# Layer 1's running maximum, taken by VectorE from each PSUM bank of scores

## The chip, the cores and the metric

The program runs on one core of a Trainium2 chip. A core has five engines that run their own instruction queues in order: TensorE (PE; its weight loads are listed apart as PEld), VectorE (DVE), ScalarE (ACT), GpSimd (POOL) and SyncE (SP, which here only issues DMAs). TensorE writes into PSUM, eight banks of 512 fp32 numbers on each of 128 partitions; VectorE and ScalarE read it. The metric is the device time of one execution in microseconds, the median of several runs.

## The reference, cut to what matters

Four layers follow each other on an image batch of shape (4, 64, 64, 128): a 7x7 neighbourhood attention, a full attention, a gated projection with a layer norm, and a selective scan in four directions. The change touches the second, "layer 1":

```python
def _L1_conv_ref(x, gn_scale, gn_bias, wq, bq, wk, bk, wv, bv, wo, bo):
    B, H, W, C = x.shape
    N = H * W
    h = group_norm(x, gn_scale, gn_bias)
    hf = h.reshape(B, N, C)
    q = hf @ wq + bq
    k = hf @ wk + bk
    v = hf @ wv + bv
    w_ = jnp.einsum('bqd,bkd->bqk', q, k) * C ** (-0.5)
    w_ = jax.nn.softmax(w_, axis=2)
    o = jnp.einsum('bqk,bkd->bqd', w_, v)
    o = o @ wo + bo
    return x + o.reshape(B, H, W, C)
```

With N = 4096 positions per image, the scores are a 4096 x 4096 matrix per image. Everything is fp32. The softmax over the keys needs the largest score of each query.

## The kernel before, in words

The function `layers_0_to_2` goes through the four images one after the other. Per image it runs layer 0, then layer 1 with layer 2 and the front of layer 3 woven into it; `layer_3` follows at the end for all images.

Layer 1 (the function `layer_1`) takes 32 blocks of 128 queries. The scores of a block are held transposed: keys on the partitions, queries along the free dimension, 32 key tiles of 128 x 128 in one SBUF tile `st` (L606). They are made in eight groups of four key tiles. For a group, `score` lets TensorE do four matmuls (L613) into one PSUM bank `ps`, and ScalarE copies the bank into `st` (L616). The banks come from a ring of four (`ps_s`), which layer 2's and layer 3's matmuls share.

The maximum of each query over all keys is found in steps:

- VectorE takes the elementwise maximum over key tiles in SBUF, once four groups are there: tiles 0 to 7 against 8 to 15 at group 3 (L618), then the running maximum `mx` of eight tiles against the next eight at groups 5 and 7 (L620).
- `fold` brings the eight tiles down to one with three maxima of 512, 256 and 128 elements (L625).
- `soften` lets TensorE transpose that tile (L630, into `pt`). VectorE reduces it to minus the maximum of each query (L632, `nm`), multiplies the identity by it (L634, `dm`), and TensorE multiplies a matrix of ones with that (L636, into `pb`), which gives a bank in which every partition has minus the maximum of each query. VectorE adds it to `st` in two halves (L639) and ScalarE takes the exponential of each (L640).

`value` multiplies the exponentials with the values, whose extra column of ones gives the sum (L646), and `finish` divides and adds to `xt` (L650, L651).

The loop over i runs three blocks at once: it makes the scores of block i, softens block i-1, and takes the values of block i-2. `fold` of block i-1 stands at the head of iteration i, `soften` ahead of group 2. Behind each block, `between(i)` adds a slice of layer 2 (four kinds of slice in turn: `turn`, `mix`, `add`, `norm`, L685 to L747) and of the front of layer 3 (projections L786, gates L815, convolution taps on ScalarE, GpSimd and VectorE, L829 to L865, and more). So a cycle of four blocks repeats. TensorE's stream in a block is, group by group, four score matmuls and four value matmuls.

The order on each engine isn't simply the order of the calls: except where `keep_in_program_order` pins an instruction, the framework's scheduler arranges each engine's queue, and it adds the waits between engines. It also keeps two engines from one PSUM bank.

Of the kernel before, what the change touches and what calls it, by code (L numbers as in the profile page):

```python
# [22 lines left out]
F32 = mybir.dt.float32  # L23
AF = mybir.ActivationFunctionType
ALU = mybir.AluOpType
# [4 lines left out]
P = 128  # L30
B, H, W, C = 4, 64, 64, 128
L = H * W
NT = L // P
# [105 lines left out]
def layers_0_to_2(  # L139
    ctx, tc, xf, mata, matb, rows, rpb, convw, sel, ident, cl, dram, big, ring, early, x3_d, ub_d, zf_d, y_d, dbl_d, ct_d, gw_d, bw_d  # L140
):
    nc = tc.nc
    wp = ctx.enter_context(tc.tile_pool(name="wa", bufs=1))
    tmp = ctx.enter_context(tc.tile_pool(name="tmp", bufs=2))
# [5 lines left out]
    def ps_s(shape, name):  # L150
        return psp.tile(shape, F32, name=name, tag="s", bufs=4)

    def ps_t(shape, name):
        return psp.tile(shape, F32, name=name, tag="t", bufs=2)

    def ps_o(shape, name):
        return psp.tile(shape, F32, name=name, tag="o", bufs=2)
# [11 lines left out]
    def m(name, p=P):  # L169
        a, e = MA[name]  # L170
        return ma[0:p, a:e] if e <= nma else once[0:p, a - nma:e - nma]
# [73 lines left out]
    ones = wp.tile([P, P], F32, name="ones")  # L245
# [308 lines left out]
    def layer_1(b, xt, hT, st, between):  # L554
        mv = sml.tile([P, 2], F32, name="mv1", tag="mv1", bufs=1)
        nc.vector.bn_aggr(mv, st)

        pm = ps_o([P, 1], "pm")
        nc.tensor.matmul(pm, lhsT=m("group"), rhs=mv[:, 0:1], start=True, stop=True)
        gm = sml.tile([P, 1], F32, name="gm", tag="gm", bufs=1)  # L560
        nc.vector.tensor_copy(gm, pm)
        dv = sml.tile([P, 1], F32, name="dv", tag="dv", bufs=1)
        nc.vector.tensor_tensor(dv, mv[:, 0:1], gm, ALU.subtract)
        vv = sml.tile([P, 1], F32, name="vv", tag="vv", bufs=1)
        nc.vector.scalar_tensor_tensor(vv, dv, dv, mv[:, 1:2], ALU.mult, ALU.add)
        pvar = ps_o([P, 1], "pvar")
        nc.tensor.matmul(pvar, lhsT=m("group"), rhs=vv, start=True, stop=True)
        sd = sml.tile([P, 1], F32, name="sd", tag="sd", bufs=1)
        nc.vector.tensor_scalar(sd, pvar, 1e-6, None, ALU.add)
        nc.scalar.activation(sd, sd, AF.Sqrt)  # L570
        ga = sml.tile([P, 1], F32, name="ga", tag="ga", bufs=1)
        nc.vector.reciprocal(ga, sd)
        nc.vector.tensor_tensor(ga, ga, cl("gn_s"), ALU.mult)

        qT = big.tile([P, L], F32, name=f"qT1_{b}", tag="qT")
        kT = big.tile([P, L], F32, name=f"kT1_{b}", tag="kT")

        v = big.tile([P, NT, C + 1], F32, name=f"v1_{b}", tag="v")
        nc.gpsimd.memset(v[:, :, C:C + 1], 1.0)
        for n in range(NCH):  # L580
            cs = bass.ts(n, CH)
            nc.vector.tensor_scalar(hT[:, cs], hT[:, cs], gm, ga, ALU.subtract, ALU.mult)
            pq = ps_s([P, CH], "pq1")
            nc.tensor.matmul(pq, lhsT=m("wq"), rhs=hT[:, cs], start=True, stop=True)
            nc.scalar.activation(qT[:, cs], pq, AF.Identity, bias=bqk[:, 0:1], scale=C ** -0.5)
            pk = ps_s([P, CH], "pk1")
            nc.tensor.matmul(pk, lhsT=m("wk"), rhs=hT[:, cs], start=True, stop=True)
            nc.scalar.activation(kT[:, cs], pk, AF.Identity, bias=bqk[:, 1:2])
            pv = ps_s([P, 4, C], "pv1")
            for k in range(4):  # L590
                nc.tensor.matmul(pv[:, k, :], lhsT=hT[:, bass.ts(4 * n + k, P)], rhs=wvo, start=True, stop=True)
            nc.vector.tensor_tensor(
                v[:, 4 * n:4 * n + 4, 0:C], pv, vrow.unsqueeze(1).to_broadcast([P, 4, C]), ALU.add
            )

        G = 4

        class Block:
            pass

        def start(i):
            k = Block()
            k.st = ring([P, NT, P], "st")  # L606
            k.mx = tmp.tile([P, 2 * G, P], F32, name="mx1", tag="mx1")
            return k

        def score(i, k, g):  # L610
            ps = ps_s([P, G, P], "sc1")
            for r in range(G):
                nc.tensor.matmul(  # L613
                    ps[:, r, :], lhsT=kT[:, bass.ts(G * g + r, P)], rhs=qT[:, bass.ts(i, P)], start=True, stop=True
                )
            nc.scalar.copy(k.st[:, G * g:G * g + G, :], ps)  # L616
            if g == 3:
                nc.vector.tensor_tensor(k.mx, k.st[:, 0:8, :], k.st[:, 8:16, :], ALU.max)  # L618
            elif g in (5, 7):
                nc.vector.tensor_tensor(k.mx, k.mx, k.st[:, 4 * g - 4:4 * g + 4, :], ALU.max)  # L620

        def fold(k):
            mx = k.mx
            for n in (4, 2, 1):
                nc.vector.tensor_tensor(mx[:, 0:n, :], mx[:, 0:n, :], mx[:, n:2 * n, :], ALU.max)  # L625

        def soften(k):
            mx = k.mx
            pt = ps_t([P, P], "pt1")
            nc.tensor.transpose(pt, mx[:, 0, :], ident)  # L630
            nm = sml.tile([P, 1], F32, name="nm1", tag="nm1")
            nc.vector.tensor_reduce(nm, pt, AX.X, ALU.max, negate=True)  # L632
            dm = tmp.tile([P, P], F32, name="dm1", tag="dm1")
            nc.vector.tensor_scalar(dm, ident, nm, None, ALU.mult)  # L634
            pb = ps_t([P, P], "pb1")
            nc.tensor.matmul(pb, lhsT=ones, rhs=dm, start=True, stop=True)  # L636
            for h in range(2):
                part = k.st[:, 16 * h:16 * h + 16, :]
                nc.vector.tensor_tensor(part, part, pb.unsqueeze(1).to_broadcast([P, 16, P]), ALU.add)  # L639
                nc.scalar.activation(part, part, AF.Exp)  # L640

        def value(k, g):
            if g == 0:
                k.po = ps_o([P, C + 1], "po1")
            for j in range(G * g, G * g + G):
                nc.tensor.matmul(k.po, lhsT=k.st[:, j, :], rhs=v[:, j, :], start=(j == 0), stop=(j == NT - 1))  # L646

        def finish(i, k):
            ri = sml.tile([P, 1], F32, name="ri1", tag="ri1")
            nc.vector.reciprocal(ri, k.po[:, C:C + 1])  # L650
            nc.vector.scalar_tensor_tensor(xt[:, i, :], k.po[:, 0:C], ri, xt[:, i, :], ALU.mult, ALU.add)  # L651

        blocks = {}
        for i in range(NT + 2):
            if 0 < i <= NT:
                fold(blocks[i - 1])
            if i < NT:
                blocks[i] = start(i)
            for g in range(NT // G):

                if 0 < i <= NT and g == (2 if i < NT else 0):
                    soften(blocks[i - 1])
                if i < NT:
                    score(i, blocks[i], g)
                if i >= 2:
                    value(blocks[i - 2], g)
            if i >= 2:
                finish(i - 2, blocks.pop(i - 2))
            between(i)
# [440 lines left out]
    for b in range(B):  # L1110
# [5 lines left out]
        def between(i):  # L1116

            n, part = divmod(i - 6, 4)
            if i == 6 and b + 1 < B:
                ahead.append(load_x(b + 1))  # L1120
            if i >= 6 and n < NCH:
                parts[part](n)
            first_part(i)
            if b + 1 < B and i == NT + 1:
                edge_of[b + 1] = edge_bias(0)
            if b + 1 < B and i == NT + 3:
                bias_m[:] = bias_tiles()
                for t, d in zip(bias_m, bias_d):
                    nc.sync.dma_start(t, d)

        first_part = front(b)
        first_part(-1)
        layer_1(b, xt, *handed.pop(b), between)
        if b + 1 < B:
            coming = layer_0(b + 1, ahead[0], edge_of[b + 1])
# [385 lines left out]
```

## Time and profile before

| | us |
|---|---|
| median of 3 runs | 3769.5 (3767.92 to 3772.58) |
| the profiled execution | 3760.92 |
| its span, first to last instruction | 3759.1 |
| VectorE's maxima of 1024 elements, L618: 128 of them | 162.1 |
| the folds L625: 384 of them, 655 ns mean | 251.5 |
| the score matmuls L613, first to last | 233.9 to 3037.2 |

The mean granted clock of TensorE was 0.921 of full speed, and 0.98 to 1.00 in the stretches of layer 1. The chain of work that ended last, by engine and by line:

```profile
PE 53%; DVE 22%; ACT 9%; POOL 6%; issue 6%; DMA 3%; SPq 1%; DVEq 0%; POOLq 0%; ACTq 0%
PE po L646 14%; PE sc L613 14%; DVE mx L625 4%; PE pt L493 4%; DVE acc L865 3%; POOL inp L1242 3%; DVE st L639 3%; PE sc L458 2%; PE po L504 2%; DVE mx L620 2%; POOL y L1284 2%; ACT st L640 2%; ACT st L616 2%; PE pp L514 1%; PE pz L815 1%
```

The rows of groups have the line, the engine, the operation, what it writes and reads, the shapes and the count; behind the first bar the busy time in us and the mean duration in ns; behind the second the time for which the engine stood idle ahead of these instructions, and what ended most of that. TensorE matmuls overlap each other, so their rate is read from the starts: eight records of 128 columns (four fp32 matmuls, each of two records) take 0.89 us. The trace has five stretches: the four images with layers 0 to 2 up to about 3060 us, each with its layer 1 of some 520 to 550 us, and layer 3 behind them.

### The profile page before, as it was taken

To read this page: it belongs to the slowest core of one execution; us is meant where nothing else is said; L and a number is where in the kernel's file an instruction comes from. 1 tells how busy PE (TensorE), PEld (TensorE's weight loads), DVE (VectorE), ACT (ScalarE), POOL (GpSimd) and SP (SyncE) were. 2 spreads that over 40 slices of the span, in tenths; PEclk is the share of its full clock that TensorE was granted. 3 is DMA by queue.
4 is the path that set the end of the run, shared out by engine and by line. 5 is a ranking of instruction groups with operands and counts; after the bars stand their busy time and mean duration, and the time that the engine had idled before them with its cause. 6 is when DMAs were issued, how large, how long until landed. Compare 5 with 4: busy or idle time off the path is not lost.

```text
span 3759.1 us, 69275 instructions
## 1 busy us (share of the span) xinstructions
PE 3353.6 (89%) x26774; PEld 2764.6 (74%) x26774; DVE 2812.2 (75%) x4843; ACT 2697.4 (72%) x4385; POOL 1447.7 (39%) x1592
## 2 busy tenths in 40 slices
PE   6999999999999999998999999989999987666647
PEld 3779989966799889667998897779988862222236
DVE  3667777766777788666777876667777867999968
ACT  3865667778676776786677777867767768999934
POOL 5500012245122122451222223522221337999856
PEclk8999999999999999999999999999999995555569
DMA  4100000131010012410121212100100259999998
GB/s 139 52 3 27 10 18 30 44 100 36 18 43 32 32 41 81 129 42 4 48 75 32 72 44 97 45 1 24 46 27 32 68 153 241 222 227 205 214 265 289
DMA packets 188301, 310.89 MB, mean 83 GB/s; under 512 B 22303, under 2 KB 110908, under 8 KB 183068
## 3 DMA queue, kind: packets, MB, share of 16 engines
q1 hardware_dynamic: 144068, 220.79, 17.4%
q0 software_dynamic: 24384, 76.95, 11.4%
q10 hardware_dynamic: 19520, 8.73, 0.8%
q8 instruction: 211, 3.46, 0.4%
q14 instruction: 118, 0.97, 0.1%
HBM read 167.69 MB, written 155.56 MB: 86 GB/s over the span
## 4 chain that ended last, share of the span: by engine, by line
PE 53%; DVE 22%; ACT 9%; POOL 6%; issue 6%; DMA 3%; SPq 1%; DVEq 0%; POOLq 0%; ACTq 0%
PE po L646 14%; PE sc L613 14%; DVE mx L625 4%; PE pt L493 4%; DVE acc L865 3%; POOL inp L1242 3%; DVE st L639 3%; PE sc L458 2%; PE po L504 2%; DVE mx L620 2%; POOL y L1284 2%; ACT st L640 2%; ACT st L616 2%; PE pp L514 1%; PE pz L815 1%
## 5 line engine op out<-in xcount | busy, mean ns | idle before, releaser
L646 PE MATMUL po<-v,st 128*128 128x129 f32 x8192 | 1076.3, 274 | 4.1 <-ACT st L640 4.1
L613 PE MATMUL sc<-qT,kT 128*128 128x128 f32 x8192 | 1075.6, 275 | 0.4 <-ACT st L616 0.4
L613 PEld LDWEIGHTS sc<-qT,kT 128*128 128x128 f32 x8192 | 997.7, 192 | 21.9 <-issue 19.0
L646 PEld LDWEIGHTS po<-v,st 128*128 128x128 f32 x8192 | 993.9, 191 | 5.4 <-issue 5.4
L616 ACT COPY st<-sc 128x512 f32<-128x512 f32 x1024 | 577.8, 583 | 499.4 <-PE sc L613 491.2
L639 DVE TENSOR_TENSOR st<-st,pb 128x2048 f32<-128x2048 f32 x256 | 573.8, 2282 | 46.2 <-PE pb L636 45.7
L620 DVE TENSOR_TENSOR mx<-mx,st 128x1024 f32<-128x1024 f32 x256 | 317.9, 1242 | 240.5 <-ACT st L616 238.4
L640 ACT ACTIVATE st<-st 128x2048 f32<-128x2048 f32 x256 | 482.7, 1908 | 9.5 <-DVE st L639 8.2
L1231 PE MATMUL pdt<-dbl,dt 8*128 8x512 f32 x512 | 307.3, 1081 | 144.1 <-ACT de L1238 141.9
L1242 POOL TENSOR_TENSOR inp<-de,ub 128x1024 f32<-128x1024 f32 x128 | 410.1, 4406 | 10.6 <-DMA ub_d<-u 6.4
L1231 PEld LDWEIGHTS pdt<-dbl,dt 8*128 8x128 f32 x512 | 114.2, 312 | 334.3 <-ACT de L1238 269.9
L710 POOL TENSOR_TENSOR x<-x,row 128x512 f32<-128x512 f32 x32 | 50.0, 1561 | 736.8 <-PE pt L275 736.8
L484 POOL TENSOR_SCALAR pr<-pr,sm 128x308 f32<-128x308 f32 (+3 forms) x512 | 243.6, 495 | 220.5 <-DVE sm L482 188.5
L856 POOL TENSOR_TENSOR gsum<-gsum,tp 128x504 f32<-128x504 f32 (+1 forms) x177 | 251.0, 1420 | 141.5 <-ACT gsum L844 81.5
L476 ACT ACTIVATE pr<-pr,mx 128x308 f32<-128x308 f32 (+3 forms) x512 | 262.6, 517 | 0.0
L625 DVE TENSOR_TENSOR mx<-mx 128x512 f32<-128x512 f32 (+2 forms) x384 | 251.5, 655 | 5.9
L1269 DVE TENSOR_TENSOR_SCAN h<-h,end,inp 128x1024 f32<-128x1024 f32 x96 | 221.1, 2346 | 19.2 <-ACT h L1255 8.7
L462 DVE CUSTOM_DVE_ANT_0 pr<-sc,bias_m 128x266 f32<-128x266 f32 (+1 forms) x384 | 152.0, 452 | 109.6 <-PE sc L458 103.6
L493 PE MATMUL pt<-ident,pr 128*88 128x128 f32 (+5 forms) x1472 | 203.5, 275 | 7.8 <-ACT prT L495 7.8
L1284 POOL DMA_DIRECT2D y<-yo x112 | 201.4, 2725 | 10.5 <-DVE yo L1283 7.9
L865 DVE SCALAR_TENSOR_TENSOR acc<-xh,cc,acc 128x512 f32<-128x512 f32 (+3 forms) x250 | 200.9, 833 | 2.2 <-ACT acc L829 1.6
L493 PEld LDWEIGHTS pt<-ident,pr 128*88 128x88 f32 (+5 forms) x1472 | 163.4, 138 | 44.9 <-ACT prT L495 31.6
(234 smaller groups left out, 5249.1 us busy)
## 6 DMA issues: line engine op xcount, KB each, us to landing
y<-yo POOLq DMA_DIRECT2D x112, 512.0 KB, 10.6
y<-y SPq DMA_DIRECT2D x48, 512.0 KB
zf_d<-zf SPq DMA_DIRECT2D x64, 256.0 KB
ub_d<-u SPq DMA_DIRECT2D x64, 256.0 KB
ub<-ub_d SPq DMA_DIRECT2D x16, 1024.0 KB
yl<-y SPq DMA_DIRECT2D x64, 256.0 KB
zc<-zf_d SPq DMA_DIRECT2D x64, 256.0 KB
x<-in_x SPq DMA_DIRECT2D x128, 64.0 KB
```

Source lines behind the costliest of these rows:

```text
L493: pin(nc.tensor.transpose(pt[0:n, h, :], k.pr[:, h, at:at + n], ident))
L613: nc.tensor.matmul(ps[:, r, :], lhsT=kT[:, bass.ts(G * g + r, P)], rhs=qT[:, bass.ts(i, P)], start=True, stop=True)
L616: nc.scalar.copy(k.st[:, G * g:G * g + G, :], ps)
L620: nc.vector.tensor_tensor(k.mx, k.mx, k.st[:, 4 * g - 4:4 * g + 4, :], ALU.max)
L625: nc.vector.tensor_tensor(mx[:, 0:n, :], mx[:, 0:n, :], mx[:, n:2 * n, :], ALU.max)
L639: nc.vector.tensor_tensor(part, part, pb.unsqueeze(1).to_broadcast([P, 16, P]), ALU.add)
L640: nc.scalar.activation(part, part, AF.Exp)
L646: nc.tensor.matmul(k.po, lhsT=k.st[:, j, :], rhs=v[:, j, :], start=(j == 0), stop=(j == NT - 1))
L865: nc.vector.scalar_tensor_tensor(acc, x, c, acc, ALU.mult, ALU.add)
L1231: nc.tensor.matmul(pdt[j][:, g, :], lhsT=dt[o:o + RANK, P * f:P * f + P], rhs=at(dbl[o:o + RANK, :], k & 2, g0, g0 + CH), start=True, stop ...
L1242: nc.gpsimd.tensor_tensor(by_rows(inp), by_rows(de), at(ub_s[f], b ^ (k & 1), SC * n, SC * n + SC), ALU.mult)
L1284: nc.gpsimd.dma_start(here if f == 1 and k == 3 else there, yo, accum_op=ALU.add)
```

## The change

The running maximum covers four key tiles instead of eight, and VectorE takes each group from its PSUM bank when it comes, rather than from `st`. At group 1 it takes the first group from `st` and the second from its bank; at groups 2 to 7 the running maximum and the bank. One fold of 512 elements is dropped. `soften` is cut in two: `turn_maxima` (the transpose, the reduction, the multiplication with the identity) stays ahead of group 2, and the rest, from the product with ones on, comes ahead of group 3. Behind the last block both come at group 0 as before. ScalarE's copy of each group stays.

```diff
-            k.mx = tmp.tile([P, 2 * G, P], F32, name="mx1", tag="mx1")
+            k.mx = tmp.tile([P, G, P], F32, name="mx1", tag="mx1")
...
             nc.scalar.copy(k.st[:, G * g:G * g + G, :], ps)
-            if g == 3:
-                nc.vector.tensor_tensor(k.mx, k.st[:, 0:8, :], k.st[:, 8:16, :], ALU.max)
-            elif g in (5, 7):
-                nc.vector.tensor_tensor(k.mx, k.mx, k.st[:, 4 * g - 4:4 * g + 4, :], ALU.max)
+            if g > 0:
+
+                nc.vector.tensor_tensor(k.mx, k.st[:, 0:G, :] if g == 1 else k.mx, ps, ALU.max)
...
-            for n in (4, 2, 1):
+            for n in (2, 1):
                 nc.vector.tensor_tensor(mx[:, 0:n, :], mx[:, 0:n, :], mx[:, n:2 * n, :], ALU.max)
...
-        def soften(k):
-            mx = k.mx
+        def turn_maxima(k):
             pt = ps_t([P, P], "pt1")
-            nc.tensor.transpose(pt, mx[:, 0, :], ident)
+            nc.tensor.transpose(pt, k.mx[:, 0, :], ident)
             nm = sml.tile([P, 1], F32, name="nm1", tag="nm1")
             nc.vector.tensor_reduce(nm, pt, AX.X, ALU.max, negate=True)
-            dm = tmp.tile([P, P], F32, name="dm1", tag="dm1")
-            nc.vector.tensor_scalar(dm, ident, nm, None, ALU.mult)
+            k.dm = tmp.tile([P, P], F32, name="dm1", tag="dm1")
+            nc.vector.tensor_scalar(k.dm, ident, nm, None, ALU.mult)
+
+        def soften(k):
             pb = ps_t([P, P], "pb1")
-            nc.tensor.matmul(pb, lhsT=ones, rhs=dm, start=True, stop=True)
+            nc.tensor.matmul(pb, lhsT=ones, rhs=k.dm, start=True, stop=True)
...
                 if 0 < i <= NT and g == (2 if i < NT else 0):
+                    turn_maxima(blocks[i - 1])
+                if 0 < i <= NT and g == (3 if i < NT else 0):
                     soften(blocks[i - 1])
```

## The prediction

> **What bounds the kernel now.** I read the sum of busy times first, then the waits of TensorE, then one cycle of layer 1 block by block, and last the VectorE timeline at the end of a block. Of the page, the busy line and four groups:
>
> ```profile
> PE 3353.6 (89%) x26774; PEld 2764.6 (74%) x26774; DVE 2812.2 (75%) x4843; ACT 2697.4 (72%) x4385; POOL 1447.7 (39%) x1592
> ...
> L616 ACT COPY st<-sc 128x512 f32<-128x512 f32 x1024 | 577.8, 583 | 499.4 <-PE sc L613 491.2
> L639 DVE TENSOR_TENSOR st<-st,pb 128x2048 f32<-128x2048 f32 x256 | 573.8, 2282 | 46.2 <-PE pb L636 45.7
> L620 DVE TENSOR_TENSOR mx<-mx,st 128x1024 f32<-128x1024 f32 x256 | 317.9, 1242 | 240.5 <-ACT st L616 238.4
> ```
>
> TensorE is the fullest engine, and in layer 1 it is nearly full: the scores (L613) and the products with the values (L646) are issued every 0.89 us per four tiles. ScalarE waits for TensorE and VectorE for ScalarE, so neither is short of time on average. What TensorE itself waits for in layer 1 stands in the view of waits:
>
> ```profile
> DVE nm L632 <- PE pt L630: 147.8, 111, 3.9
> ...
> PE pt L630 <- DVE mx L625: 66.1, 67, 2.2
> ...
> PE pb L636 <- DVE dm L634: 17.6, 16, 2.5
> ```
>
> The columns are us in total, times, and the longest. TensorE stands still 66.1 us ahead of the transpose of the maxima (L630) and 17.6 us ahead of the product with ones (L636): 83.7 us, 2.2% of the span, is the plain ceiling of this change. 67 waits, three to a cycle of four blocks, make 22 such cycles. The four rows of one of them, each from one transpose L630 to the next:
>
> ```profile
> core 0: us, PE busy (x) PEld busy (x) DVE busy (x) ACT busy (x) POOL busy (x), PEclk, DMA share, GB/s
> 1094.10:1113.30 19.20, 18.31 (x162) 16.68 (x162) 18.74 (x29) 14.97 (x21) 3.57 (x4) 1.00 0.04 10
> 1113.30:1130.60 17.30, 15.54 (x136) 15.19 (x137) 14.22 (x18) 12.99 (x18) 4.86 (x4) 1.00 0.23 81
> 1130.60:1147.40 16.80, 15.42 (x136) 15.16 (x137) 12.96 (x13) 9.55 (x13) 4.74 (x4) 1.00 0.06 19
> 1147.40:1166.10 18.70, 18.55 (x142) 16.48 (x143) 11.33 (x14) 15.09 (x20) 3.45 (x3) 1.00 0.08 29
> ```
>
> The first block is VectorE's (18.74 of 19.20 us: it also carries the convolution taps L865 and layer 2's statistics). The fourth is TensorE's. The second and third are neither's: a chain of latencies through three engines bounds them. That chain, at the end of the third block, on VectorE:
>
> ```profile
> 1141.75 1.23 DVE L620 TENSOR_TENSOR mx<-mx,st 128x1024 f32<-128x1024 f32 x1 [1.24 <-ACT st L616]
> 1142.89 0.16 DVE L650 RECIPROCAL ri<-po 128x1 f32<-128x1 f32 x1
> 1143.01 1.66 DVE L625 TENSOR_TENSOR mx<-mx 128x512 f32<-128x512 f32 x1
> 1144.59 0.34 DVE L651 SCALAR_TENSOR_TENSOR x<-po,ri,x 128x128 f32<-128x128 f32 x1
> 1144.85 0.67 DVE L689 TENSOR_REDUCE rs<-x2T 128x8 f32<-128x512 f32 x1
> 1145.44 1.88 DVE L625 TENSOR_TENSOR mx<-mx 128x256 f32<-128x256 f32 x2
> 1147.74 0.29 DVE L632 TENSOR_REDUCE nm<-pt 128x1 f32<-128x128 f32 x1 [0.42 <-PE pt L630]
> ```
>
> The last copy of scores ends at 1141.71; the maximum and three folds then take until 1147.32. The timeline of TensorE shows L630 at 1147.38 with 1.38 us idle ahead of it: it could have begun at 1146.0.
>
> **The change, part by part.**
>
> *The maxima.* Per block, VectorE loses one L618 (1267 ns), two L620 (1242) and the 512-wide fold (917 by its own form row): 4.67 us. It gains seven 512-wide maxima of a PSUM bank and an SBUF tile. No row is a maximum of that kind. The nearest is L592, an addition of a PSUM bank and SBUF, 128x512, at 691 ns; L719, the same kind, has 681. From below, the shortest 512-wide L625 took 626 ns; from above, 691 plus the 104 ns that a chained L620 leaves after its predecessor makes 795. I take 691, the row: 7 x 0.691 = 4.84 us, so +0.17 us a block and +22 us of VectorE over 128 blocks (ends -37 and +115). In light blocks, where VectorE is idle 147.8 us ahead of L632 alone, this costs nothing; in the 22 heavy blocks it is 22 x 0.17 = 4 us on the path. L639, also half from PSUM, never takes longer than 2290 ns, while the SBUF-only L625 of 512 spreads from 626 to 1659, so I count no stretched case for the new maxima; the 256 and 128 folds keep theirs.
>
> *The end of the chain, third block.* After the last copy at 1141.71 there now come one maximum 0.69, the 256 fold 0.42, the reciprocal, L651 and L689 (about 0.26 + 0.60 + 0.08 in their spacing), and the 128 fold, 0.29 undisturbed or 1.23 as here: 1144.1 to 1145.1, ahead of 1146.0. The 1.38 us goes entirely; TensorE's own next work is then the bound. Gain 1.4.
>
> *The banks.* A score bank was free after ScalarE's copy; now it is free after copy and maximum. In the changed program's order, each maximum waits for ScalarE's copy of its bank, and 426 of the 1024 score groups wait for VectorE by name. No row shows two engines reading one bank. The Trainium skill, "PSUM — Partial Sum Buffer", section "PSUM bank collisions raise a hardware error", says ScalarE and VectorE may not access one bank at once, reads included, and speaks against the hope that copy and maximum run side by side: by it a bank is held 0.58 + 0.69 = 1.27 us at least, and the last maximum begins after the copy. Were they parallel, every chain would be 0.58 us shorter, up to 0.58 x 44 = 26 us for second and third blocks. I take the serial reading, as the program's waits do. Four banks at one group per 1.79 us give about 7 us of run-ahead, against VectorE's longest stretch without a maximum, two L639 of 4.5 us. In a light block: L639 starts 0.5 us after the product with ones, the maximum of group 3 ends 5.7 us after it, and group 7, which takes its bank, comes 7.2 us after it. Cover 1.5 us; each us that L639 starts later than 2 us after the product costs a us.
>
> *The product with ones, a group later.* It now follows a score group and a value group (1.8 us) behind the transpose instead of 0.9. nm and dm (0.29 + 0.29 to 0.53, plus hand-overs of 0.42 and 0.03) are done 1.1 to 1.3 us after the transpose; where the next block's first maximum is queued ahead of nm it adds 0.7: still about in time. So most of the 17.6 us goes. In return L639, the exponentials L640 behind it, and the copies behind those come about 0.9 us later. Values need the exponentials only a block later, so TensorE doesn't see it there. But in the second block ScalarE loads a table (1.28) and does both exponentials (3.71) between copies; four copies then follow in a row, and the maxima behind them. Walking the second block from the timeline: the copies of groups 4 to 6 began at 1124.27, now about 1125.2; the maximum of group 4 ends near 1125.9, and TensorE wants that bank at 1125.2. It loses about 1 us there, and of the 1.62 us that it lost ahead of L630 (at 1130.57) 0.6 is left as gain.
>
> *First block.* VectorE's queue from nm to the last fold took 18.77 us. With the maxima between the taps at spacing 0.6 (0.69 less the 0.08 overlap of independent neighbours) the new queue is 0.2 longer, but one tap (0.66) is now ordered behind the last fold: 0.4 shorter. Bank waits ahead of the layer-2 and convolution matmuls cost TensorE some of it. Gain 0.3. *Fourth block:* TensorE bound; 0.2 from the product with ones.
>
> *The rest.* No DMA is added, moved past or removed on SP's or POOL's queue; ScalarE gets two more table loads (2.6 us, in its slack); the other layers' orders on the engines are the same.
>
> **Sum:** 22 cycles x (0.3 + 0.6 + 1.4 + 0.2) = 55 us; the first blocks of three batches, which stall 1 to 3 us at the same two lines, give about 1 each: 58. The profiled execution took 3760.9 us around its span of 3759.1, and 3760.9 - 58 = 3703. The median of the runs, 3769.5, is 8.6 above it, so I predict 3769.5 - 58 = 3711.
>
> **Rivals.**
> 1. *Forecast: the stalls ahead of L630 and L636 mostly go.* 3711, own range 3680 to 3745. Chance 0.53.
> 2. *Nearly everything goes*, because the later product never delays a copy and stretched folds become rare: 83.7 us plus 0.6 in 22 heavy blocks, about 97: 3673. For it: the wide fold loses about 30 us to stretching today (917 ns mean against 0.68 us in undisturbed timeline entries, 128 times). Against: the heavy block's 18.74 us. Chance 0.11.
> 3. *The wait only moves*, from L630 to the score groups (L613), which wait for banks. The 2.5 us of a cycle are then eaten by 1 us each in the first and second block and 0.5 in the third: 3769. For it: today only 0.4 us of L613's idling is for a copy, so nothing in the trace tests the banks. Chance 0.12.
> 4. *Slower: the banks put VectorE into TensorE's path.* Place: heavy and second blocks. In the second of the cycle above L639 began at 1117.01, 2.4 us after the product at 1114.65, and my walk of the heavy one puts it 1.6 after. If taps, layer 2's normalisation (L734, up to 1.44 us each) and the two adds stand ahead of maximum 3, or the table load and exponentials ahead of the copies, TensorE loses about 3 us in each of the 44 such blocks, 132 us, against 22 x 1.4 = 31 and 17 saved elsewhere: 3769.5 + 84 = 3854; at 2 us a block it is 3810. It decides from about 1.1 us per such block, since 44 x 1.1 = 48. Chance 0.24.
>
> What a measurement of this kernel can tell from no change is 0.2%, 7.5 us. Faster: 0.53 + 0.11 and a little of 3, 0.65; same 0.10; slower 0.25. The range takes in case 2 and the near part of 4: 3668 to 3785.
>
> **What would show it.** Right: TensorE's wait at the transpose falls from 66 us to below 20, that at the product from 17.6 to below 10, the third block takes 15.4 us instead of 16.8, and VectorE's busy time rises by about 20 us. Wrong: a new row in which score matmuls wait for the maxima by more than 40 us, a first block above 20 us, a 512-wide maximum well above 0.7 us, or a stall ahead of the product because nm stands behind a maximum that waits for a copy.

## The result, and the profile after

| | before | after |
|---|---|---|
| median, us (4 runs each) | 3771.04 (3767.92 to 3773.55) | 3719.79 (3716.71 to 3723.46) |
| ratio, 95% interval | | 0.9868 (0.9856 to 0.988) |
| the profiled execution, us | 3760.92 | 3719.04 |
| its span, us | 3759.1 | 3717.3 |
| mean granted clock of TensorE | 0.921 | 0.916 |

The change takes 51 us off, 1.3%. The forecast was 3711, a gain of 58. The clock is a little lower after, so it is no part of the gain. The traced execution of the kernel before took 10 us less than its median, so the two traces differ by only 41.9 us: what is read from them below accounts for 42 us, not for 51. Of the page after, the busy line and the rows of the copies, the new maxima and the addition of the product; columns as explained above:

```profile
PE 3357.8 (90%) x26774; PEld 2775.6 (75%) x26774; DVE 2794.8 (75%) x5227; ACT 2700.4 (73%) x4387; POOL 1422.9 (38%) x1592
...
L616 ACT COPY st<-sc 128x512 f32<-128x512 f32 x1024 | 574.8, 584 | 426.0 <-PE sc L613 425.4
L619 DVE TENSOR_TENSOR mx<-mx,sc 128x512 f32<-128x512 f32 x768 | 524.7, 683 | 201.8 <-ACT st L616 178.2
L639 DVE TENSOR_TENSOR st<-st,pb 128x2048 f32<-128x2048 f32 x256 | 574.6, 2281 | 5.2 <-PE pb L636 4.1
```

A maximum of a bank and SBUF takes 683 ns, against the 691 of the addition L592 by which it was priced, and all 896 of them lie between 669 and 691. L639 takes what it took, but VectorE idles 5.2 us ahead of it instead of 46.2: by the time that the product arrives, it has other work. TensorE's waits after, us in total, times, and the longest:

```profile
PE pb L636 <- DVE dm L632: 24.6, 34, 1.9
...
PE sc L613 <- DVE mx L619: 15.6, 8, 3.3
...
PE pt L628 <- DVE mx L624: 6.7, 4, 2.0
...
PE pi L788 <- DVE mx L619: 3.8, 3, 1.3
```

The transpose's 66.1 us (now line L628) are down to 6.7. The product's 17.6 didn't fall, they rose to 24.6. And two rows are there that had no counterpart before: the score matmuls wait 15.6 us for a maximum, because that holds a bank, and layer 3's projections, which use the same ring of banks, wait 3.8. Of the 15.6 us, 12.4 are one wait at the start of each of the four images.

Now the cycle shown before, block by block from one transpose to the next; columns as in the same view before:

```profile
1088.70:1107.20 18.50, 18.50 (x161) 16.75 (x160) 16.91 (x32) 13.37 (x18) 2.26 (x2) 1.00 0.01 2
1107.20:1123.30 16.10, 15.32 (x137) 15.13 (x135) 13.21 (x22) 14.55 (x21) 6.24 (x5) 1.00 0.29 99
1123.30:1138.50 15.20, 15.20 (x138) 15.16 (x137) 12.33 (x16) 9.26 (x12) 3.29 (x3) 1.00 0.07 19
1138.50:1158.50 20.00, 18.46 (x143) 16.39 (x141) 11.80 (x17) 15.18 (x21) 4.24 (x4) 1.00 0.07 27
```

First, second and third block went from 19.2, 17.3 and 16.8 to 18.5, 16.1 and 15.2: TensorE is busy through the first and third from end to end. The fourth block of this cycle lost 1.3 (20.0; it is 18.7 in the next cycles), with a wait of 1.5 us at the product, and the first block behind it takes 20.9 where it took 18.4. That pair comes once in each of the last three images, 3 x (1.3 + 2.5) = 11 us in all.

One cycle isn't typical: the second blocks of the kernel before last between 14.9 and 19.6 us. So here are all stretches from one transpose to the next in the two traces, 31 in each image, summed by their place; the first three of an image stand outside the cycles:

| | forecast, us | gained, us |
|---|---|---|
| 28 first blocks (the forecast counts 22 cycles) | 22 x 0.3 = 6.6 | 1.3 |
| 28 second blocks | 22 x 0.6 = 13.2 | 13.3 |
| 28 third blocks | 22 x 1.4 = 30.8 | 34.9 |
| 28 fourth blocks | 22 x 0.2 = 4.4 | -4.0 |
| the starts of the images | 3 | -5.3 |
| sum | 58 | 40.2 |

The remaining 1.7 of the 41.9 us lie outside these stretches.

One number of the page doesn't fit the forecast's picture at all. VectorE was to be busy about 20 us longer, and is busy 17.4 us less. The durations of its instructions, added up, rise by 7.8 us (3083.9 to 3091.6), and the rest is neighbours that overlap in time, which the page counts once. Three groups account for nearly all of it: the maxima together with the dropped wide fold +15, the multiplication with the identity +15 (410 to 527 ns), layer 2's normalisation L734 (now L736) -19 (557 to 410 ns). The instructions of the last two groups are the same in both kernels. Why the same instruction takes another time beside other work became the question.

### The profile page after: what moved, and what is told of

The parts are those of the page before. It is cut to its first block, busy times and chain, and to the rows that moved or that the text cites. A ratio compares the mean times of both kernels' runs of the same rounds, so it can differ in the third digit from the quotient of the medians.

```text
span 3717.3 us, 70142 instructions
## 1 busy us (share of the span) xinstructions
PE 3357.8 (90%) x26774; PEld 2775.6 (75%) x26774; DVE 2794.8 (75%) x5227; ACT 2700.4 (73%) x4387; POOL 1422.9 (38%) x1592
## 3 DMA queue, kind: packets, MB, share of 16 engines
q1 hardware_dynamic: 144068, 220.79, 17.6%
## 5 line engine op out<-in xcount | busy, mean ns | idle before, releaser
L613 PE MATMUL sc<-qT,kT 128*128 128x128 f32 x8192 | 1083.8, 276 | 15.6 <-DVE mx L619 15.6
L619 DVE TENSOR_TENSOR mx<-mx,sc 128x512 f32<-128x512 f32 x768 | 524.7, 683 | 201.8 <-ACT st L616 178.2
L639 DVE TENSOR_TENSOR st<-st,pb 128x2048 f32<-128x2048 f32 x256 | 574.6, 2281 | 5.2 <-PE pb L636 4.1
L712 POOL TENSOR_TENSOR x<-x,row 128x512 f32<-128x512 f32 x32 | 40.8, 1275 | 695.1 <-PE pt L275 695.1
L858 POOL TENSOR_TENSOR gsum<-gsum,tp 128x504 f32<-128x504 f32 (+1 forms) x177 | 240.9, 1364 | 170.1 <-ACT tp L850 82.2
L495 ACT COPY prT<-pt 110x512 f32<-110x512 f32 (+3 forms) x240 | 139.1, 580 | 65.0 <-PE pt L493 64.0
```

Of the source, the lines that this page charges most:

```text
L613: nc.tensor.matmul(ps[:, r, :], lhsT=kT[:, bass.ts(G * g + r, P)], rhs=qT[:, bass.ts(i, P)], start=True, stop=True)
L619: nc.vector.tensor_tensor(k.mx, k.st[:, 0:G, :] if g == 1 else k.mx, ps, ALU.max)
```

## Experiments

All ratios are to the kernel before, with 95% intervals. Twelve kernels ran. The first four take the change apart; then GpSimd's work is taken away, and the order of the bank's two readers is turned round; the last four act on what those left.

### The bank alone, and the later product alone

```diff
-                if 0 < i <= NT and g == (3 if i < NT else 0):
+                if 0 < i <= NT and g == (2 if i < NT else 0):
                     soften(blocks[i - 1])
```

> The maxima from the bank alone; the product with ones stays ahead of group 2, right behind the transpose. Theory 'the shorter chain is the gain': 3720 to 3730 us, TensorE's wait ahead of the transpose below 15 us as in the changed kernel, its wait ahead of the product up from 25 to 40 us or so. Theory 'the later product carries a good part': 3740 us or more. The kernel before stands at 3771, the changed one at 3720.

Measured: 3743.44, ratio 0.9929 (0.9916 to 0.9941). The transpose waits 6.9 us, the product 43.4.

The other half: the kernel before, with `soften` split as in the change, and its maxima of eight tiles from `st` kept.

> The later product alone; the maxima stay eight tiles wide and from the SBUF copy. Theory 'the shorter chain is the gain': 3765 to 3772 us, since the wait ahead of the transpose stays near 66 us and the product is late for another reason. Theory 'the later product carries a good part': the 17.6 us ahead of the product go, 3750 to 3758 us.

Measured: 3776.47, ratio 1.0019 (1.0012 to 1.0026). The transpose waits 65.4 us, as before; the product 16.1, as before; the scores 17.2 for a copy.

What follows: the bank clears the transpose and brings 25 us alone (27 by its ratio). The later product alone loses a little (7 us by its ratio, which neither expectation had), since the transpose ahead of it is as late as ever. Together they bring 51. Without the delay, nearly half of what is gained at the transpose (59 us) is given back at the product (26 us more): the transpose is early, and `dm` isn't. By place, the later product pays in the fourth blocks: with the bank alone they lose 25.5 us on the kernel before, with both 4.0.

### Group by group, but from the copy

The changed kernel, its maxima of four tiles reading ScalarE's copy instead of the bank. The chain behind the last copy is as short as in the change; only what is read differs.

```diff
-                nc.vector.tensor_tensor(k.mx, k.st[:, 0:G, :] if g == 1 else k.mx, ps, ALU.max)
+                nc.vector.tensor_tensor(
+                    k.mx, k.st[:, 0:G, :] if g == 1 else k.mx, k.st[:, G * g:G * g + G, :], ALU.max
+                )
```

> As the changed kernel, but each group's maximum reads the SBUF copy instead of the PSUM bank, so banks are free after ScalarE's copy. If the four-tile shape alone makes the gain: 3720 us within 5. If holding the banks costs the 15.6 us of score waits: near 3705 us, and score matmuls wait below 2 us for the maxima. If reading PSUM spares VectorE the stretching beside GpSimd: the 512-wide maxima rise from 683 ns mean to 800 or more and the time to 3735 us or more.

Measured: 3775.47, ratio 1.0014 (1.0005 to 1.0022). No gain is left. In its trace, an execution 9 us above the median, the waits are 36.2 us at the product, 30.3 ahead of the scores and 16.4 at the transpose; the maxima take 704 and 787 ns in the mean, the multiplication with the identity 593, and VectorE is busy 2904 us, 109 more than in the changed kernel. The shorter chain does its part at the transpose, 16.4 us for 66.1, but the product and the scores take that back: 36.2 us for `dm` and 8.0 behind a reciprocal, less the 17.6 of before, plus 30.3 make 57, against 50 saved. This run has a flaw: without the bank's waits the scheduler also places some of VectorE's instructions otherwise. The trace shows where that falls. By place, first and third blocks gain on the kernel before (18.5 and 33.9 us), as in the change, but the second blocks lose 50.8. There four of layer 2's normalisations stand ahead of the addition of the product, and GpSimd works beside them:

```profile
1121.71 3.95 DVE L738 TENSOR_SCALAR x<-x,mv,rd 128x128 f32<-128x128 f32 x4
1121.73 0.46 PE L638 MATMUL pb<-dm,ones 128*128 128x128 f32 x2
...
1125.58 2.27 DVE L641 TENSOR_TENSOR st<-st,pb 128x2048 f32<-128x2048 f32 x1
```

The product is done at 1122.2, and the addition starts 3.4 us later; in other second blocks it is up to 5.2, in the changed kernel mostly 0.1. Against the changed kernel the second blocks alone lose 64 us in the traces, so the 56 us to it lie there, where order and stretching act together. How much each would cost alone isn't shown.

### The multiplication with the identity on ScalarE

```diff
-            nc.vector.tensor_scalar(k.dm, ident, nm, None, ALU.mult)
+            nc.scalar.activation(k.dm, ident, AF.Copy, scale=nm)
```

> As the changed kernel, but ScalarE multiplies the identity by minus the maximum instead of VectorE (527 ns mean there, 280 ns where undisturbed). Theory 'the product waits because that instruction is stretched beside GpSimd': TensorE's wait ahead of the product falls from 24.6 us to below 10 and the time to 3700 to 3712 us. Rival 'it waits because its queue is late': ScalarE's queue is as late, the wait stays above 20 us and the time at 3718 us or more.

Measured: 3712.65, ratio 0.9846 (0.9832 to 0.9859), 7 us below the changed kernel, where the two intervals just touch. The product's wait lies between the two expectations: it is 13.2 us instead of 24.6, and the scores' wait for a maximum 25.3 instead of 15.6: ScalarE's copies come a little later, and the banks with them. Part of the product's wait is the time that VectorE takes for `dm`, then. The timeline of the changed kernel shows why it takes it (start, duration, both in us):

```profile
1108.57 1.26 POOL L858 TENSOR_TENSOR gsum<-gsum,tp 128x504 f32<-128x504 f32 x1 [1.53 <-ACT tp L850]
1108.64 1.27 DVE L632 TENSOR_SCALAR dm<-ident,nm 128x128 f32<-128x128 f32 x1
...
1110.06 0.46 PE L636 MATMUL pb<-dm,ones 128*128 128x128 f32 x2 [0.78 <-DVE dm L632]
```

An instruction of 0.29 us elsewhere lasts 1.27 us, until GpSimd's addition beside it is through (1109.83), and TensorE stands 0.78 us at the product.

### Without GpSimd's work

Three kernels with GpSimd's elementwise work in layer 2 and in the front of layer 3 cut to 8 columns each: the additions to `gsum` and `acc`, the ones to `x`, the products with `rt` and `bb`. They leave out that part of the computation. One of those cuts, the others are alike:

```diff
-                nc.gpsimd.tensor_tensor(a, a, p, ALU.add)
+                nc.gpsimd.tensor_tensor(a[:, 0, 0:8], a[:, 0, 0:8], p[:, 0, 0:8], ALU.add)
```

The kernel before, so cut:

> The kernel before with GpSimd's additions and products of layers 2 and 3 in the four images cut to eight elements each: most of the convolution's partial sums, of the gated product, of the output bias and of the product with B are left out. Their order and waits stay[...]. Port theory (the gain of reading PSUM is that the maxima aren't stretched beside GpSimd): the wide maxima and folds fall to 1.22, 0.68, 0.42 and 0.29 us and the time by 25 us or more, to 3745 or less. Bank and order theory: within 10 us of 3768.

Measured: 3654.0, ratio 0.9693 (0.968 to 0.9706).

The changed kernel, so cut:

> The changed kernel with the same work of GpSimd left out. Port theory: the rest of the stretching (dm 527 to 280 ns, the 256 fold 662 to 420) goes, TensorE's wait ahead of the product falls from 24.6 us to below 8, time 3695 to 3708 us; what then is left between this and the kernel before with the same cut is the shorter chain, 30 to 45 us. Bank and order theory: 3715 to 3722 us.

Measured: 3660.27, ratio 0.9707 (0.9694 to 0.972).

The maxima group by group from the copy, so cut:

> The variant whose maxima read the SBUF copy, with the same work of GpSimd left out. Port theory: the 55 us between it and the changed kernel close, within 8 us of the changed kernel with the same cut. Order theory (the scheduler's other order, with four normalisations ahead of the addition, is what costs): 30 us or more stay between them.

Measured: 3636.26, ratio 0.9646 (0.9633 to 0.9659).

Of the kernel before, so cut, two of the folds, in the view of groups by form:

```profile
L625 DVE TENSOR_TENSOR mx<-mx 128x512 f32<-128x512 f32 x128 | 87.7, 685 | 0.4
...
L625 DVE TENSOR_TENSOR mx<-mx 128x128 f32<-128x128 f32 x128 | 37.5, 293 | 3.4
```

These folds took 917 and 569 ns; now they take 685 and 293, and no transpose waits for them any more: the row of 66.1 us is gone from the list, and 1.5 us are left at the product. The cut relieves other instructions of VectorE too (the normalisation from 557 to 342 ns), so it doesn't single out the folds; but the order of VectorE's instructions is the same in 112 of the 124 stretches between transposes, and the stall is gone. In the kernel before, GpSimd's work beside VectorE made the stall, not the number of the chain's steps.

What it stretched isn't the same in every block. In the first and third blocks of the kernel before it is the folds: 2.40 and 3.43 us for the three in the median, 45 of the 66 us of waits, and with GpSimd's work cut 1.37 and 1.40 us and no wait. In the second blocks the folds take 1.40 us with that work and without it, yet TensorE waits 18.4 us. There, in the second block of the cycle in the prediction, two normalisations stand ahead of the addition:

```profile
1114.63 2.45 DVE L734 TENSOR_SCALAR x<-x,mv,rd 128x128 f32<-128x128 f32 x2
1114.65 0.46 PE L636 MATMUL pb<-dm,ones 128*128 128x128 f32 x2
...
1117.01 4.47 DVE L639 TENSOR_TENSOR st<-st,pb 128x2048 f32<-128x2048 f32 x2
```

In seven second blocks the addition starts 1.9 to 2.0 us behind the product, as here, and the transpose at the end of the block waits 1.6 or 1.7; in six it starts 0.9 us behind, and the wait is 0.7; of those in which it starts at once, only one has a wait, and that one has stretched folds. The exponentials and copies behind it carry the delay to the end of the chain.

Without GpSimd's work, the change gives nothing: 3660 against 3654, where 30 to 45 us had been expected. And holding the bank costs, with the order that goes with it: read from the copy, with the same short chain, the kernel is 24 us faster (3636 against 3660), where at most 8 us either way had been expected. The score matmuls' waits for a maximum, 12.4 us and again one at the start of each image, are half of that; reading the copy has none. With GpSimd's work the same comparison stands the other way round, 3775 against 3720.

### The maximum ahead of the copy

The changed kernel, with the maximum of each group issued ahead of ScalarE's copy, so that the copy waits for it.

> As the changed kernel, but the maximum stands ahead of ScalarE's copy of the same bank. If the two are kept apart on a bank, the copy now waits for the maximum: VectorE's end of the chain is 0.58 us shorter, but VectorE's two additions of 4.5 us now stand ahead of copies, and score matmuls wait for banks more than the 15.6 us of today: 3730 us or more. If the two run side by side, nothing changes or the time falls to 3705 to 3720 us.

Measured: 3733.89, ratio 0.9902 (0.9889 to 0.9916), 14 us above the changed kernel. ScalarE's copies now wait for a maximum 353 times, so the two follow each other here too. The scores wait 7.8 us for a copy and the products with the values 12.7 for an exponential; the product with ones waits 24.3 us for `dm` and 6.1 for ScalarE. Of the two readers in line at a bank, the copy is the better first one in this kernel.

### One reduction in place of the folds

If two operands from SBUF are what is stretched, a reduction with one operand should do the folds' work in a constant time. In the changed kernel:

```diff
-            for n in (2, 1):
-                nc.vector.tensor_tensor(mx[:, 0:n, :], mx[:, 0:n, :], mx[:, n:2 * n, :], ALU.max)
+            k.top = tmp.tile([P, P], F32, name="top1", tag="top1")
+            nc.vector.tensor_reduce(k.top, k.mx.rearrange("p t q -> p q t"), AX.X, ALU.max)
```

> The changed kernel, but its two folds (256 and 128 elements, both operands from SBUF) become one reduction of 512 elements to 128 with a single operand, on VectorE. Theory A (what delays TensorE at the transpose and the product is VectorE's operations with two SBUF operands, stretched beside GpSimd): a reduction of 512 elements takes 0.67 us in the row of L689 and is not stretched, against 0.66 + 0.37 us for the two folds now; the wait at the transpose goes to 0 to 3 us and the kernel takes 3705 to 3715 us, ratio 0.983 to 0.986. Theory B (the chain's length alone counts, stretching is a side effect): the undisturbed chain is 0.42 + 0.29 = 0.71 against 0.67, so nothing moves: 3720, ratio 0.987. Against both: the reduction over a stride of four tiles is slower than 0.8 us, and the time rises above 3722.

Measured: 3710.63, ratio 0.9838 (0.9825 to 0.9852), within what theory A gave. The reduction is longer than expected, 1.05 us, but all 128 of them lie between 1.01 and 1.09, where a block's two folds, added up from the trace, took 0.7 us in the median and 2.0 at the 90th percentile. What was expected of its duration was wrong, then, and so was the clause that a slow reduction would cost the gain: it is no shorter than what it replaces (0.66 + 0.37 us in the mean), only constant, and the kernel gains 9 us on the changed one. The wait at the transpose had little left to give (4.6 us for 6.7, not the 0 to 3 expected); the product's falls from 24.6 to 13.8 for `dm` and 5.5 for a copy.

With the multiplication on ScalarE as well:

> As the run above, and the identity times the maxima (L632) on ScalarE as well. Theory A: both of the chain's operations that GpSimd stretches are gone, so the waits at the transpose and the product together fall below 15 us; 3695 to 3706 us, ratio 0.980 to 0.983. Theory B: as the kernel with the multiplication on ScalarE alone, 3713, ratio 0.9846.

Measured: 3730.27, ratio 0.9889 (0.9874 to 0.9903). Both theories miss it. The two repairs don't add: the product's wait falls to 6.4 us, but the scores wait 42.5 us for maxima, and the normalisation L735 is stretched to 734 ns in the mean, against 373 in the run before.

The kernel before, with the same two edits:

> The kernel before, with its maxima of 1024 elements from SBUF as they are, but its three folds as one reduction of 1024 elements with a single operand (to 1.3 us by L620's 1.24) and the identity times the maxima on ScalarE; nothing reads a bank for longer. Theory A: the folds' stretching (251 us busy against about 1.38 x 128 = 177 undisturbed) goes and with it most of the 66 and 17.6 us ahead of the transpose and the product; the maxima themselves can still be stretched. 3725 to 3740 us, ratio 0.988 to 0.992. Theory B (the maxima's length and their place behind the copy count, which only the bank reading shortens): 3765 to 3772, ratio 0.998 to 1.0.

Measured: 3732.09, ratio 0.9895 (0.9881 to 0.9909), theory A's. Here too the normalisation is stretched, to 820 ns in the mean. Its timeline at the head of a second block, four of them beside GpSimd's additions and products:

```profile
1112.18 4.69 DVE L732 TENSOR_SCALAR x<-x,mv,rd 128x128 f32<-128x128 f32 x4
1113.04 1.27 POOL L857 TENSOR_TENSOR acc<-acc,gsum 128x512 f32<-128x512 f32 x1
...
1116.79 4.47 DVE L637 TENSOR_TENSOR st<-st,pb 128x2048 f32<-128x2048 f32 x2
```

The product is done at 1114.5, yet the addition to the scores starts at 1116.79, because four normalisations stand ahead of it and last 4.69 us. Without that edit, in the run below, the addition starts first, at 1112.62, and the four normalisations further behind last 1.11 us. In the run above, with both repairs in the changed kernel, the addition starts up to 6.2 us behind the product in the second blocks.

So the last run takes only the fold, and leaves the multiplication on VectorE:

```diff
-            for n in (4, 2, 1):
-                nc.vector.tensor_tensor(mx[:, 0:n, :], mx[:, 0:n, :], mx[:, n:2 * n, :], ALU.max)
+            k.dm = tmp.tile([P, P], F32, name="dm1", tag="dm1")
+            nc.vector.tensor_reduce(k.dm, k.mx.rearrange("p t q -> p q t"), AX.X, ALU.max)
...
-            nc.tensor.transpose(pt, mx[:, 0, :], ident)
+            nc.tensor.transpose(pt, k.dm, ident)
```

> The kernel before with one edit: its three folds become one reduction of 1024 elements with a single operand; the multiplication with the identity stays on VectorE. The run with that multiplication on ScalarE as well took 3732 us with 36.9 us of waits at the transpose. Theory A (the folds' stretching beside GpSimd makes the stalls at the transpose): the reduction takes 1.93 us each time and is never stretched, where the folds take 1.96 us in the mean but up to 4 us; most of the gain comes with this edit alone, 3728 to 3748 us, ratio 0.988 to 0.994, wait at the transpose 35 to 45 us and at the product 15 to 25. Theory B (the gain of the other run came from taking the multiplication off VectorE's chain): 3758 to 3772 us, ratio 0.996 to 1.0, wait at the transpose about 60 us.

Measured: 3713.01, ratio 0.9837 (0.9824 to 0.985), 62 us below the kernel before. That is beyond theory A's own range, as is the wait at the transpose, 14.2 us for 35 to 45, and it is more than the whole change brings, with no bank held and no product moved. Its groups by form, and two rows of its waits:

```profile
L624 DVE TENSOR_REDUCE dm<-mx 128x128 f32<-128x1024 f32 x128 | 248.4, 1940 | 0.3
```

```profile
PE pb L634 <- DVE dm L632: 23.6, 15, 3.8
...
PE pt L628 <- DVE dm L624: 14.2, 32, 1.2
```

248.4 us of reductions stand for 251.5 us of folds: VectorE's work on them has not shrunk. But every reduction lies between 1.81 and 2.00 us, while a block's three folds took 1.40 us in the median and 3.49 at the 90th percentile. The long ones were in the first and third blocks, and there this run gains on the trace of the kernel before: 23.8 and 30.7 us, against 0.0 in the second blocks. The third block shows it, to be held against the timeline in the prediction:

```profile
1138.01 1.23 DVE L620 TENSOR_TENSOR mx<-mx,st 128x1024 f32<-128x1024 f32 x1 [1.24 <-ACT st L616]
1138.76 1.61 POOL L708 TENSOR_TENSOR x<-x,row 128x512 f32<-128x512 f32 x1 [21.81 <-PE pt L275]
...
1139.27 1.99 DVE L624 TENSOR_REDUCE dm<-mx 128x128 f32<-128x1024 f32 x1
```

From the last maximum's end (1139.24) to the reduction's end (1141.26) it takes 2.0 us, beside GpSimd's work; the folds needed 4.3 (1142.98 to 1147.32). Of the 2.3 us saved, 1.5 are the folds' own length (3.54 us against 1.99), and some 0.8 come from the order: between dependent folds the scheduler had put L651 and L689, and a single reduction has no gap for them. In the first blocks the order is the larger part: the three folds add up to 2.40 us in the median but stand spread over 4.8, where the reduction takes 1.95 in one piece. The cut kernel above shows that without the stretch there is no stall, in nearly the same order; no run has the order alone.

## Why the forecast held, and where it was wrong

**The size of the gain: right**, 51 us for 58, within the range. Rivals 2 (nearly everything), 3 (the wait only moves) and 4 (slower) didn't occur. But it is in part the right sum by luck. In the traces 40 of the forecast's 58 us are there: third blocks gave more than forecast, first and fourth blocks and the starts of the images less, and the 10 us between the traced execution of the kernel before and its median no trace explains.

**The maxima: right.** 683 ns for 691, and none was stretched, as forecast from L639. Maxima of the bank added 15 us net of the wide fold, for 22 forecast.

**The end of the chain in the third block: right**, 15.1 to 15.2 us for 15.4 forecast, and 34.9 us in all for 30.8. The forecast took the 67 waits as three in each of 22 like cycles; 27 of them are in third blocks, 20 in first and 16 in second ones. Fewer steps follow the last copy, and the transpose's wait goes with them, even where the maxima read the copy. What the forecast didn't see is why the chain was too long. It noted that the wide fold loses 30 us to stretching and put that into rival 2 as a bonus; but all three folds together lose 72 (251.5 us less 128 x 1.40), and with GpSimd's work cut the same long chain makes no stall. The change cures this by room: it drops the wide fold and takes the maxima from the bank, and leaves the two short folds as stretched as they were (132 us for 134). The Trainium skill, "SBUF — State Buffer", section "Who interferes with whom", says that a VectorE instruction with two SBUF inputs contends with a GpSimd instruction that reads SBUF, that one with at most one SBUF input outside certain fast modes doesn't, that `tensor_scalar` can, and that `tensor_reduce` on trn2 never does. The runs agree row by row: maxima from the bank 683 to 685 ns with GpSimd's work or without it; folds of 128 columns 569 against 293; `dm`, a `tensor_scalar`, 527 against 286; the reductions all within 0.2 us of each other. That the cause is a port is the skill's statement; the runs show who is stretched, and beside whom.

**The second block: right in sum, for another reason**, 13.3 us for 13.2; in the cycle shown 16.1 us for the 16.7 forecast. The microsecond that the forecast lost there, for the bank of a copy behind the table load and the exponentials, doesn't appear: TensorE's only wait in that block is 0.8 us at the product. The delay of the addition by the stretched normalisations, which the forecast listed in rival 4 as a danger, was already there before. With the later product they are done when it arrives, and the addition starts 0.1 us behind it.

**The first and the fourth block and the starts: overestimated**, -8.0 us together for 14 forecast. Most first blocks gain 0.3 to 0.6. The fourth blocks gain nothing, and three lose 1.3 by a late `dm`. Behind each of these the first block loses 2.5: there a projection waits 1.3 us and a score group 0.8 for a maximum. At the start of each image the scores wait 2.6 to 3.3 us for one. Both are a piece of rival 4, at 19.4 us in all instead of 132.

**The product with ones, a group later: this step failed.** "Most of the 17.6 us goes" became 24.6. `dm` was priced at 0.29 to 0.53 us, and as done 1.1 to 1.3 us after the transpose, or 0.7 later with a maximum ahead: 2.0 at most. In the entry shown it takes 1.27 beside `gsum`, and ends 2.7 us after the transpose (1107.22 to 1109.91). The direction was right: with the bank and without the delay the wait is 43.4. What the delay buys is 24 us, 21 of them in the fourth blocks; and it buys nothing without the bank, where the transpose is late anyway.

**VectorE's busy time: wrong**, -17 for +22, as the maxima's term was the only one summed; changed stretching elsewhere and overlap took more than it added.

## What to carry to other kernels

Where VectorE works beside GpSimd, look at the spread of an instruction's durations, not at its mean alone: the folds' mean was 1.96 us and the reduction's is 1.94, and the kernel is 62 us faster, in part because one instruction also leaves no gap for others. An instruction with one SBUF operand, a reduction or one that takes its second operand from PSUM, is worth its place on the chain that TensorE waits for, even when its undisturbed time is longer. Look also at what stands ahead of such an instruction in its queue: in the second blocks here it was a few stretched normalisations that decided. Before moving data or work to shorten such a chain, try it with the neighbour's work cut down: that shows in one run whether the length or the neighbour makes the wait, and what the repair itself costs.

## What had not been expected of the hardware

- A reduction of 512 elements along a stride of 128 columns takes 1.05 us, where L691, of the same 512 elements, takes 0.67. It differs from L691 in two ways, the stride and its 128 results instead of 8, and no run separates them.
- Relief moves the stretch. With `dm` on ScalarE the changed kernel gains about 7 us, but with the reduction in place the same edit loses 20 (3710.6 to 3730.3) and on the kernel before 19 (3713.0 to 3732.1): the normalisations come to lie beside GpSimd and ahead of the addition. Which arrangement is lucky was not foreseen by any theory here.
- The best two, the reduction in the changed kernel (0.9838) and in the kernel before (0.9837), can't be told apart. With it, the reading of the bank and the later product bring nothing that can be measured.
- Still open: the share of order against stretch in the version that reads the copy, and that version with the reduction, which wasn't run.
